# Where the first batch's rotation-table pieces and output weights stand in the load queue

## The chip, the cores and the metric

The kernel runs on one core of one Trainium2 chip. The metric is the device time of one execution in microseconds (us). The engines are named as in the profile: PE is the matrix engine (PEld its weight loads), DVE the vector engine, ACT the scalar engine, POOL the GpSimd engine, SP the engine whose queue issues every DMA of this kernel, in program order.

## The reference, cut to what matters

Two layers work on an image batch `x` of shape 8 x 256 x 96 x 96 in float32. The change touches only the first layer, and only for the first batch element:

```python
# layer 0, after a group norm of x
q_f = fft2(pconv(x, w1, b1)); k_f = fft2(pconv(x, w2, b2)); v_f = fft2(pconv(x, w3, b3))
q_f, k_f = l2_normalize(q_f), l2_normalize(k_f)          # per head, over all frequencies
attn = einsum('bhcn,bhdn->bhcd', q_f, k_f) * temperature
attn = complex(softmax(real(attn)), softmax(imag(attn)))
out  = abs(ifft2(einsum('bhcd,bhdn->bhcn', attn, v_f)))
x    = x + pconv(out, w_out)
# layer 1, after another group norm of x: linear attention with softplus features, added to x
```

No transform is carried out in full. The attention needs only sums over pairs of image rows (x with itself, and x with its mirrored image), and the absolute value of the inverse transform needs each image and a rotated copy of it.

## The kernel before

Each batch element passes through five stages, which Python generators interleave into one program. The order of instructions on every engine, SP included, is the order in which they are written, since the kernel schedules by hand.

- Pair sums. `first_sums` (first batch element only) turns 12 steps of two image rows each on PE, and `pair_sums(0)` does the rest, from row group u = 6 on. A row group is loaded by `load_grouped` (eight DMAs, L161 and L163, for two row groups), transposed on DVE in `turn_blocks` (L502), stored to the DRAM buffer `xtd` (L507), added and subtracted on POOL and DVE in `pair` (L529, L530), and multiplied on PE in `products` (L458), three block steps for each row group and one for the last, u = 12. The generator `rest` is `pair_sums(0)`: after its four preparing steps it yields after each block step, so that the index i of the loop `for i, _ in enumerate(rest)` counts 19 block steps, i = 0 to 18. The last row group is transposed at L489 and L491 and stored to `xtm` (L492).
- Tables. `tables()` builds a rotation table and writes it to the DRAM buffer `rx` (L283, L284) in 13 pieces for later reading; then it prepares small constants (`gsel`, `rep4`, `sel8`, L290 to L297) and hands over to `load_small`, which loads biases and weights. The output weights `wo` are loaded there: one DMA for the first half (L230), and 16 of 8 KB each for the second (L232), four of them between two yields. `parts` is this generator; each `next(parts)` runs it to its next yield.
- Rotation. `rotate(b)` returns `fetch`, which names or loads the next row pair and, when it is the first of a piece, loads the piece of the table from `rx` into a tile `tm` (L750, 159 KB, four buffers), and a generator of 49 steps (`turns`). A step multiplies rows by the piece on PE (L795) and copies the result to an image buffer (L801, L802) on ACT or DVE in turn. A piece serves four steps. Before step i, `steps` fetches ahead to row pair i // 2 + 3, so that step 0 fetches row pairs 0 to 3 (pieces 0 and 1), step 2 piece 2, step 6 piece 3, step 10 piece 4, step 14 piece 5 and step 18 piece 6. The first 12 row pairs of the first batch element are still in SBUF from `first_sums`; from pair 12 on they are loaded from `xtd` (L781) into slots that earlier pairs leave.
- Attention. `attention(b)` is a chain of small operations that yields the number of turns to be placed between two of its links. `mix(b, chain, turns)` does that.
- Images, then the second layer (`images`, `layer1`, `output`): the products with `wo` are at L864.

In the block steps of the first batch element, two turns each are run at i = 9, 10 and 11 and one each from i = 12 on (steps 0 to 12); the remaining turns are run in `mix`.

The DMAs of SP around the change thus stand in this order: store of row groups 6 and 7, eight loads, store of 8 and 9, six small loads of the last row group (L155, L156), pieces 0 and 1, store of 10 and 11, pieces 2 and 3, the store to `xtm`, the small loads, the weights `wl` (L452), five loads of `wo`, piece 4, twelve loads of `wo`, pieces 5 and 6, row pairs from `xtd`.

Of the kernel before, what the change touches and what calls it, by code (L numbers as in the profile page):

```python
# [73 lines left out]
def two_layer_kernel(ctx: ExitStack, tc: tile.TileContext, x, w1t, b1, w2t, b2, w3, b3, wot, temp,  # L74
# [139 lines left out]
    def load_small():  # L214
        nc.gpsimd.memset(b12[0:64], 0.0)
        yield
        for c, v in enumerate((b1, b2)):
            for m in range(KC):
                nc.sync.dma_start(out=b12[32 * m:32 * m + 1, c, :], in_=v[m * P:(m + 1) * P].unsqueeze(0))
        yield  # L220
        for c, v in enumerate((bk, bq)):
            nc.sync.dma_start(out=bkq4[:, c:c + 1], in_=bass.AP(v.tensor, v.offset, [[0, 4], [1, 32], [1, 1]]))
        for k in range(KC):
            nc.sync.dma_start(out=tcol[:, k:k + 1], in_=bass.AP(temp.tensor, temp.offset + 4 * k, [[1, 4], [0, HEAD], [1, 1]]))
        yield
        for c, v in enumerate((wkt, wqt)):
            nc.sync.dma_start(out=wkq0[:, :, c, :], in_=v.rearrange("(k p) o -> p k o", p=P))
        nc.sync.dma_start(out=b3col, in_=b3.rearrange("(k p) -> p k", p=P))
        yield
        nc.sync.dma_start(out=wo[:, 0, :], in_=bass.AP(wot.tensor, wot.offset, [[C, 16], [HEAD * C, NH], [1, C]]))  # L230
        for j in range(16):
            nc.sync.dma_start(out=wo[NH * j:NH * j + NH, 1, :], in_=wo_v[HEAD - j if j else 16])  # L232
            if j % 4 == 3:
                yield


    csn = const.tile([P, 3, H], F32, name="csn")
# [17 lines left out]
    def tables():  # L255
# [40 lines left out]
        nc.vector.tensor_copy(sel8.rearrange("p (i d) -> p i d", d=D), rep4[:, 0:8].unsqueeze(2).to_broadcast([P, 8, D]))  # L296
        nc.vector.tensor_scalar_mul(csn[:, 0:2, N + 1:H], csn[:, 0:2, N + 1:H], -1.0)  # L297
        yield from load_small()

    def tm_tile(name):  # L300
# [35 lines left out]
    def finish(stage):  # L336
        for _ in stage:
            pass
# [19 lines left out]
    def first_loads():  # L358

        nc.sync.dma_start(out=t0[:, 0:2 * W], in_=tmat[0, :, W:3 * W])  # L360
        x0 = x_of(0)

        def load(lo, hi):
            o = LO if hi <= H // 2 else 0
            nc.sync.dma_start(out=x0[:, :, o + lo * W:o + hi * W], in_=x_v[0, :, :, lo * W:hi * W])

        for lo, hi in ((0, 4), (H - 4, H), (4, 8), (H - 8, H - 4), (8, 16), (H - 16, H - 8)):
            load(lo, hi)
        yield
        load(16, 2 * NU)  # L370
        yield
        load(H - 2 * NU + 1, H - 16)
        load_grouped(0, V0)
        yield
        load_grouped(0, V0 + 1)
        yield
# [338 lines left out]
    def b3_part(b):  # L715

        pg = ps_tile(f"b3_{b}")
        mz, nmean, at = m0.pop(b)
        atf = at.rearrange("p m n h -> p m (n h)")
        for c in range(3):  # L720
            for j, r in enumerate(blocks(c)):
                for k in range(KC):
                    nc.tensor.matmul(pg[r, c:c + 1], lhsT=columns(atf, k, c, j), rhs=b3col[:, k:k + 1],
                                     start=(c == 0 and k == 0), stop=(k == KC - 1), skip_group_check=True)
        beta = one.tile([P, 3], F32, tag="beta", name=f"beta_{b}")
        nc.vector.tensor_copy(beta, pg[:, 0:3])
        m0[b] = mz, nmean, beta
# [372 lines left out]
    def weave(stage, other):  # L1100

        due = 0
        for n in stage:
            due += n
            while due >= 1:
                next(other, None)
                due -= 1
# [68 lines left out]
                        next(mixed)  # L1176
                        next(mixed)

    def mix(b, chain, turns):

        for n in chain:
            for _ in range(n):
                next(turns, None)
                yield
        nc.vector.tensor_copy(y1[b][:, :, H:H + 1], m0[b][1].unsqueeze(2))
        for _ in turns:
            yield
        b3_part(b)

    E = mybir.EngineType  # L1190
    with tc.manual_schedule(engines={E.PE, E.DVE, E.Pool, E.SP, E.Activation}):
        sums, rest, loads, parts = first_sums(), pair_sums(0), first_loads(), tables()
        fetch, turns = rotate(0)
        next(loads)
        next(parts)
        next(loads)
        next(parts)
        next(loads)
        next(parts)
        finish(loads)  # L1200
        for i, _ in enumerate(sums):
            if NU - 5 < i < NU:
                next(rest)
        for i, _ in enumerate(rest):
            if i > 11:
                next(parts, None)
            for _ in range(2 if i in (9, 10, 11) else 1 if i > 11 else 0):
                next(turns)
        finish(parts)
        finish(mix(0, attention(0), turns))  # L1210
        for b in range(B):
            sums = pair_sums(b + 1) if b + 1 < B else iter(())
            weave(images(b), sums)
            weave(layer1(b), sums)
            if b + 1 < B:
                fetch, turns = rotate(b + 1)
                mixed = mix(b + 1, attention(b + 1), turns)
                output(b, *l1.pop(b), fetch, sums, mixed)
                finish(mixed)
            else:  # L1220
                output(b, *l1.pop(b))
# [50 lines left out]
```

## Time and profile before

| | |
|---|---|
| median of 3 runs | 2518.16 us (2516.88 to 2520.02) |
| the profiled execution | 2517.75 us |
| its span | 2516.0 us |
| PE busy | 2476.9 us (98%) |
| PE busy from 0 to 149 us, all that precedes the images of the first batch element | 132.88 us |
| PE busy from 149 to 2420 us | 2263.96 of 2271 us |
| mean granted PE clock from 0 to 149 us | 0.95 of full speed |

The profile is one execution. A time such as 70.5 counts from the start of its span. PE, DVE, ACT and POOL times are those of instructions; SP times are those of issuing a DMA, which moves its data later. A remark in brackets behind an instruction is the time for which its engine stood idle before it, and what ended that. The program order on each engine is fixed[...].

### The profile page before, as it was taken

To read this page: it belongs to the slowest core of one execution; us is meant where nothing else is said; L and a number is where in the kernel's file an instruction comes from. 1 tells how busy PE (TensorE), PEld (TensorE's weight loads), DVE (VectorE), ACT (ScalarE), POOL (GpSimd) and SP (SyncE) were. 2 spreads that over 40 slices of the span, in tenths; PEclk is the share of its full clock that TensorE was granted. 3 is DMA by queue.
4 is the path that set the end of the run, shared out by engine and by line. 5 is a ranking of instruction groups with operands and counts; after the bars stand their busy time and mean duration, and the time that the engine had idled before them with its cause. 6 is when DMAs were issued, how large, how long until landed. Compare 5 with 4: busy or idle time off the path is not lost. (4 is left out here: it accounts for less than half of the span.)

```text
span 2516.0 us, 41727 instructions
## 1 busy us (share of the span) xinstructions
PE 2476.9 (98%) x15788; PEld 1745.1 (69%) x15788; DVE 1777.8 (71%) x3450; ACT 1148.2 (46%) x2007; POOL 856.6 (34%) x806
## 2 busy tenths in 40 slices
PE   9899999999999999999999999999999999999998
PEld 8775768667685667856678566785677757777546
DVE  5467776687856877578775787757876577766776
ACT  2244364443545445354453535435354453634553
POOL 5024513245133442144331452413524136142311
PEclk9899999999999999999999999999999999999997
DMA  9544619356292653916559263683638627296004
GB/s 242 152 154 105 174 64 331 139 137 174 72 336 93 168 143 118 339 63 158 135 173 327 49 166 97 230 271 63 163 86 284 216 63 197 53 318 207 1 7 151
DMA packets 274786, 403.79 MB, mean 160 GB/s; under 512 B 39670, under 2 KB 202906, under 8 KB 274586
## 3 DMA queue, kind: packets, MB, share of 16 engines
q1 hardware_dynamic: 274586, 401.11, 54.3%
q8 instruction: 126, 2.06, 0.4%
q14 instruction: 74, 0.61, 0.1%
HBM read 251.90 MB, written 149.14 MB: 159 GB/s over the span
## 5 line engine op out<-in xcount | busy, mean ns | idle before, releaser
L856 PE MATMUL z<-arena,mz 128*128 128x384 f32 (+1 forms) x2304 | 591.9, 488 | 0.0
L906 POOL TENSOR_TENSOR e<-e 128x768 f32<-128x768 f32 x192 | 348.4, 1814 | 552.6 <-ACT e L905 525.8
L864 PE MATMUL po<-e,wo 128*128 128x384 f32 x1536 | 527.5, 487 | 1.6 <-ACT e L907 1.6
L856 PEld LDWEIGHTS z<-arena,mz 128*128 128x128 f32 (+1 forms) x2304 | 310.1, 163 | 234.7 <-issue 50.5
L864 PEld LDWEIGHTS po<-e,wo 128*128 128x128 f32 x1536 | 290.0, 190 | 204.6 <-ACT e L907 7.2
L458 PEld LDWEIGHTS acc<-eo 128*128 128x128 f32 (+1 forms) x2224 | 353.2, 190 | 81.6 <-issue 32.3
L901 DVE TENSOR_TENSOR e<-z,xT 128x768 f32<-128x768 f32 x384 | 361.1, 949 | 66.0 <-PE z L856 65.8
L458 PE MATMUL acc<-eo 128*128 128x257 f32 (+3 forms) x2224 | 400.0, 330 | 0.0
L795 PEld LDWEIGHTS y<-tm,arena 96*128 96x128 f32 x3072 | 363.6, 193 | 49.8 <-issue 34.5
L795 PE MATMUL y<-tm,arena 96*128 96x128 f32 x3072 | 382.5, 279 | 11.4 <-DMA tm<-rx 11.4
L905 ACT ACTIVATE e<-e 128x1536 f32<-128x1536 f32 x192 | 284.4, 1481 | 174.4 <-DVE e L901 172.5
L866 DVE TENSOR_TENSOR arena<-arena,po 128x384 f32<-128x384 f32 x384 | 209.2, 551 | 181.2 <-PE po L864 181.2
L907 ACT ACTIVATE e<-e 128x768 f32<-128x768 f32 x192 | 161.9, 843 | 380.6 <-POOL e L906 376.7
L529 POOL TENSOR_TENSOR eo<-arena 128x768 f32<-128x768 f32 x83 | 172.1, 2074 | 433.2 <-DVE arena L502 332.7
L1161 POOL TENSOR_TENSOR arena<-arena,po 128x384 f32<-128x384 f32 x180 | 178.0, 1008 | 197.5 <-ACT po L1160 153.2
L801 ACT COPY arena<-y 128x384 f32<-128x384 f32 (+1 forms) x200 | 94.5, 473 | 259.6 <-PE y L795 240.8
L801 DVE COPY arena<-y 128x384 f32<-128x384 f32 (+1 forms) x192 | 104.6, 545 | 144.2 <-PE y L795 142.8
L304 DVE BATCH_NORM_STATS2 st<-arena 128x6 f32<-128x384 f32 x384 | 195.1, 548 | 0.6
L502 DVE STREAM_TRANSPOSE arena<-arena 128x768 f32<-128x768 f32 x180 | 166.1, 955 | 8.9 <-DMA xtd<-arena 7.0
L1160 ACT COPY po<-o 128x384 f32<-128x384 f32 x180 | 78.0, 482 | 191.8 <-PE o L1152 186.8
L1021 PE MATMUL xT<-ident,arena 128*128 128x128 f32 x1152 | 144.1, 275 | 1.3 <-ACT xT L1024 1.3
L1021 PEld LDWEIGHTS xT<-ident,arena 128*128 128x128 f32 x1152 | 127.1, 141 | 19.0 <-issue 16.5
(244 smaller groups left out, 2540.6 us busy)
## 6 DMA issues: line engine op xcount, KB each, us to landing
arena<-in_x_dram SPq DMA_DIRECT2D x99, 768.0 KB
out_dram<-arena SPq DMA_DIRECT2D x192, 384.0 KB
xtd<-arena SPq DMA_DIRECT2D x45, 1536.0 KB
arena<-xtd SPq DMA_DIRECT2D x180, 384.0 KB
arena<-in_x_dram SPq DMA_DIRECT2D x353, 192.0 KB
tm<-rx SPq DMA_DIRECT2D x96, 159.0 KB
wl<-in_w1t_dram SPq DMA_DIRECT2D x8, 256.0 KB
wl<-in_w2t_dram SPq DMA_DIRECT2D x8, 256.0 KB
```

The lines of the kernel that those rows point to most:

```text
L304: nc.vector.bn_stats(out=st[:, k, c, :], in_=x_of(b)[:, k, c * CH:(c + 1) * CH])
L458: nc.tensor.matmul(acc[c][:, m * (C + 1):m * (C + 1) + C + 1 - m * P], lhsT=eo[0:np_, q, c, 1 + m * P:1 + (m + 1) * P], rhs=eo[0:np_, q, c ...
L795: nc.tensor.matmul(pu[:, o:o + P], lhsT=xt[:, s, k * P:(k + 1) * P], rhs=tm[:, n:n + P], start=True, stop=True)
L801: copy(y[:, :, :, g:g + nr, :], v.rearrange("p k r (f w) -> p k f r w", f=2))
L856: nc.tensor.matmul(out[:, 0:CH].rearrange("p (h q) -> p h q", q=PR), lhsT=columns(mz, k, c, j), rhs=yz[:, k, f, :, o:o + PR], start=(k == ...
L864: nc.tensor.matmul(po[:, 0:CH], lhsT=wo[:, k, m * P:(m + 1) * P], rhs=e[:, k, :], start=(k == 0), stop=(k == KC - 1))
L866: nc.vector.tensor_add(x[:, m, n], x[:, m, n], po[:, 0:CH])
L901: nc.vector.tensor_add(e[:, 2 * c:2 * c + 2, :].rearrange("p t (q h) -> p t q h", h=H), pz[:, 0:CH].rearrange("p (h q) -> p q h", h=H).uns ...
L905: nc.scalar.activation(e, e, AF.Square)
L906: nc.gpsimd.tensor_add(e[:, 0:2, :], e[:, 0:2, :], e[:, 2:4, :])
L1021: nc.tensor.transpose(pt[:, j * C + k * P:j * C + (k + 1) * P], x[:, k, o:o + P], ident)
L1161: nc.gpsimd.tensor_add(x[:, m, r], x[:, m, r], t)
```

## The change

Three edits, none of which changes what is computed. The fetching of the first four row pairs, and with them of table pieces 0 and 1, is placed after the first block step (i = 0), where before it came with the first turn at i = 9. `load_small` yields after each of the 16 small loads of `wo` and not after every fourth. `parts` begins one block step later (i = 13), and what is left of it after the block steps is run inside `mix`, one `next(parts)` for each turn, where before it was run to its end ahead of `mix`.

```diff
         for j in range(16):
             nc.sync.dma_start(out=wo[NH * j:NH * j + NH, 1, :], in_=wo_v[HEAD - j if j else 16])
-            if j % 4 == 3:
-                yield
+            yield
...
-    def mix(b, chain, turns):
+    def mix(b, chain, turns, parts=iter(())):
 
         for n in chain:
             for _ in range(n):
                 next(turns, None)
+                next(parts, None)
                 yield
...
         for i, _ in enumerate(rest):
-            if i > 11:
+            if i == 0:
+                for _ in range(4):
+                    fetch()
+            if i > 12:
                 next(parts, None)
             for _ in range(2 if i in (9, 10, 11) else 1 if i > 11 else 0):
                 next(turns)
+        finish(mix(0, attention(0), turns, parts))
         finish(parts)
-        finish(mix(0, attention(0), turns))
```

## The prediction

> **What bounds the kernel now.** I read the page's busy times first, then PE's waits over the whole span, then the order of work on PE and on the SP queue between 55 and 112 us, then windows over the stretches where PE stops.
>
> The page and PE's waits (columns: us in total, times, longest):
>
> ```profile
> PE 2476.9 (98%) x15788; PEld 1745.1 (69%) x15788; DVE 1777.8 (71%) x3450; ACT 1148.2 (46%) x2007; POOL 856.6 (34%) x806
> ...
> PE y L795 <- DMA tm<-rx: 11.4, 3, 6.8
> PE pcs L259 <- POOL xo L424: 3.6, 1, 3.6
> PE gm_b L316 <- DVE mv_b L310: 2.7, 1, 2.7
> ```
>
> PE is busy for all but 39 us. The largest wait is that of the rotation's matmuls for pieces of the rotation table (tm): three times, 11.4 us together. They are on PE's timeline:
>
> ```profile
> 59.77 3.89 PE L458 MATMUL acc<-eo 128*128 128x257 f32 x23
> 70.50 2.90 PE L795 MATMUL y<-tm,arena 96*128 96x128 f32 x12 [6.84 <-DMA tm<-rx]
> 73.19 1.94 PE L458 MATMUL acc<-eo 128*128 128x257 f32 x8
> ...
> 94.42 3.73 PE L795 MATMUL y<-tm,arena 96*128 96x128 f32 x32
> 98.74 2.92 PE L795 MATMUL y<-tm,arena 96*128 96x128 f32 x24 [0.59 <-DMA tm<-rx]
> ...
> 107.13 5.98 PE L795 MATMUL y<-tm,arena 96*128 96x128 f32 x32 [4.02 <-DMA tm<-rx]
> ```
>
> The SP queue shows why the pieces are late (start, duration, transfer, how many):
>
> ```profile
> 56.95 1.57 SPq L163 DMA_DIRECT2D arena<-in_x_dram  x1
> 58.62 0.40 SPq L507 DMA_DIRECT2D xtd<-arena  x1
> ...
> 65.00 3.98 SPq L750 DMA_DIRECT2D tm<-rx  x2
> ...
> 91.98 1.53 SPq L232 DMA_DIRECT2D wo<-in_wot_dram  x4
> 93.62 0.79 SPq L750 DMA_DIRECT2D tm<-rx  x1
> 94.45 5.79 SPq L232 DMA_DIRECT2D wo<-in_wot_dram  x12
> 100.34 1.25 SPq L750 DMA_DIRECT2D tm<-rx  x2
> ```
>
> Pieces 0 and 1 are issued at 65.0, after PE already stands (63.66), and behind a 1.5 MB store (xtd) and six small loads. Piece 4 stands behind five wo loads, piece 5 behind twelve more. Each gap also costs clock:
>
> ```profile
> 67.00:70.50 3.50, 0.00 (x0) 0.03 (x1) 0.89 (x1) 0.00 (x0) 2.60 (x2) 0.54 0.38 88
> 70.50:74.00 3.50, 3.50 (x14) 3.36 (x15) 0.56 (x3) 0.54 (x2) 0.00 (x0) 0.50 0.12 43
> 104.90:108.30 3.40, 1.17 (x5) 1.20 (x6) 0.00 (x0) 0.00 (x0) 0.00 (x0) 0.50 0.82 193
> 108.30:111.70 3.40, 3.40 (x18) 3.40 (x17) 0.63 (x2) 0.54 (x2) 0.00 (x0) 0.50 0.21 34
> ```
>
> The third number from the right is the granted clock: 0.50 from about 67.3 to 74.1 and from about 104.9 to 111.7.
>
> [...] the second fall came 1.75 us after PE stopped, in a window that had been about half busy. [...] The window 69:72, where only tm moves, has DMA share 0.20[...]. [...]
>
> **The change, part by part.** A piece of 159 KB moves at 68 to 88 GB/s: 2.2 us.
>
> *First pieces at the head of the block steps.* The four fetches come after block step 0 of row 6: on SP just behind the eight loads that end at 58.52, ahead of the store at 58.62. Two DMAs move; the other two fetches only name tiles. Nothing is added. The source rx was written from 30 to 36 us. SP waits here fit a rule that a transfer waits for the eighth before it (the second tm waited 2.4 us for the xtd store, eight places earlier), so pieces 0 and 1 wait for the first two of the eight loads, done by about 59: issue at 58.7 and 59.2. [...] whose bytes end between 63 and 64 (DMA share 1.16 at 207 GB/s in 58:63; DVE's wait for them ends at 64.60). Then 2.2 us, then about 0.4 to the start of PE: 65.5 to 66.5. I take 66.0. The gap from 63.66 shrinks from 6.84 to 2.3: **4.5 us gained**, between 3.0 and 6.8. Piece 1 lands near 68; it is needed 6 us after piece 0.
>
> What is pushed back: the xtd store by two issues (about 1.5 us)[...]. Then the six small loads, whose reader runs on DVE at 83[...]. What else is due: row 10's sums need eo, made on POOL from 66.97 to 69.55 and untouched; PE would want it 7.5 us after it starts again, at 73.5. Covered.
>
> *Clock after the first gap.* The first group ran 12 matmuls in 2.90; at full clock 8 take 1.06 and each further 0.111, so 1.50: loss 1.40. The next eight products took 1.94 instead of 1.48: 0.46. Together 1.86. With 2.3 us of idle the clock may or may not fall[...] (idle of 1.75 in one window was enough at 104.9). I take half: **0.9 gained**, between 0 and 1.86.
>
> *wo one per turn.* Ahead of piece 4 went wo's first load and four more, 91.33 to 93.62: 2.29 us; they leave, and the small loads go one step later. The transposes of the last block also pass in front of the twelve gsel copies and six more DVE instructions (L290 to L297, 81.47 to 83.31, 1.84 us), so the xtm store on which SP waited until 83.84 comes earlier. Piece 4 is thus 4.1 us earlier against PE; it was 0.59 late. Ahead of piece 5, 5.89 us of wo (94.45 to 100.34) become one load of 0.61 and three of 0.48, 2.05: 3.84 more, 8.0 in all, against 0.59 + 4.02 of lateness. **0.59 and 4.02 gained**, and with them the half clock at 107.13: 32 matmuls in 5.98, where 94.42 has 3.73 for as many: **2.25 gained**.
>
> The other wo loads lie between later turns, 0.48 on SP for each turn of at least 1.06 us on PE. From turn 22 on SP waits for PE (row loads into slots that PE frees); seven wo between turns 20 and 26 delay those by at most 3.4 us, and such a row, issued at 110.52, is read near 117.8 with about 3 us of transfer: some 4 us of cover. First reader of wo is at 160, over 40 us later. The copies moved one step (gsel, read at 142.9; b12, at 114.2) are early enough; without that cover they would cost their 1.9 us on DVE. The chain of attention keeps its place: at 102.83 its last small matmul, 1.5 us later its result, and four turns (4.2 us) before PE needs it.
>
> Sum: 4.5 + 0.9 + 0.59 + 4.02 + 2.25 = 12.3 us. The profiled execution took 2517.75 (span 2516.0 and 1.75 around it), so 2505.4; the median shown is 0.4 higher: **2505.8**. From 149 to 2420 us PE is busy for 2264 of 2271, so what is gained at the head should reach the end whole.
>
> **Rivals.**
> - *The wait moves to piece 2.* [...] PE wants it 13.2 us after it starts again (70.50 to 85.58, less 1.86), at 79. For it: the margin is one microsecond[...]. Against it: piece 3 is not needed before 87. Two microseconds late and a halved clock cost 3 to 4: 2509.5.
> - *The first pieces land no earlier in effect*[...]: only the second part pays, 6.86: 2511.3. Against it, nothing but the eight loads is ahead of them.
> - *The chain takes the gaps' place, no change:* its waits would have to take 12 us; the 1.5 us above against 4.2 speaks against it.
> - *Slower:* wo loads in the turns hold SP while row loads queue behind; each of the eleven row loads from 110 us on would come late. It decides from 4 us of delay per load; 2 us late at all eleven, each with a piece of half clock, would be 22 + 4, less 12: 2532. Only seven wo are left by then, and SP stands idle in its waits for PE (26 us of them), which speaks against it.
>
> **Chances.** Forecast 0.62; wait at piece 2 0.19; second part alone 0.11; no change 0.04; slower 0.04. The forecast's own range is 2502 (first gap all gone with its clock: 15.6 gained, 2502.6) to 2508; to hold the rivals of the same sign it goes to 2512. A measurement tells about 0.2%, 5 us, from no change: faster 0.92, same 0.04, slower 0.04.
>
> **What would show it.** PE's wait L795 for tm falls from 11.4 to 2 or 3 us, in one piece near 64; on SP, two tm issues near 59 ahead of the xtd store, wo loads one by one between tm and row loads; clock 1.00 from 104 on. Wrong: a wait for tm at PE's step 8 (near 79 us), a wait for xtd rows after 105, or a first gap that stays over 4 us.

## The result, and the profile after

The changed kernel takes 2504.23 us (median of 4 runs, 2503.14 to 2505.93) beside 2517.52 us for the kernel before: the ratio is 0.9947, with a 95% interval of 0.993 to 0.9964, or 13.3 us less. The profiled execution of the changed kernel has a span of 2502.6 us, 13.4 us less than that of before. In the changed file the lines behind the loads of wo (L232) are one lower, so that L794 is the rotation's matmul, L749 the load of a table piece and L506 the store of a row group.

PE's waits over the whole span of the changed kernel (us in total, times, longest):

```profile
PE pcs L258 <- POOL xo L423: 3.6, 1, 3.6
...
PE y L794 <- DMA tm<-rx: 1.8, 1, 1.8
```

Three waits of 11.4 us for table pieces have become one of 1.8. On PE's timeline of the changed kernel:

```profile
65.97 1.73 PE L794 MATMUL y<-tm,arena 96*128 96x128 f32 x12 [1.85 <-DMA tm<-rx]
67.49 2.78 PE L457 MATMUL acc<-eo 128*128 128x257 f32 x8
70.06 2.24 PE L794 MATMUL y<-tm,arena 96*128 96x128 f32 x16
...
80.97 1.06 PE L794 MATMUL y<-tm,arena 96*128 96x128 f32 x8
...
89.81 6.42 PE L794 MATMUL y<-tm,arena 96*128 96x128 f32 x56
...
97.54 3.82 PE L794 MATMUL y<-tm,arena 96*128 96x128 f32 x32
101.29 1.03 PE L589 MATMUL qkm<-wl,dmm 128*2 128x256 f32 x8
```

Read it for three things. The first turn starts at 65.97 after a gap of 1.85 us. The group behind it is slow (2.78 where 1.48 is usual). From 89.81 on there is no gap at all: 56 matmuls in one line where the kernel before had 32, a wait and 24, and the 32 at 97.54 take 3.82 instead of 5.98. The SP queue of the changed kernel:

```profile
59.22 1.67 SPq L749 DMA_DIRECT2D tm<-rx  x2
60.99 0.42 SPq L506 DMA_DIRECT2D xtd<-arena  x1
...
86.00 0.80 SPq L749 DMA_DIRECT2D tm<-rx  x1
86.85 0.59 SPq L230 DMA_DIRECT2D wo<-in_wot_dram  x1
87.49 1.74 SPq L232 DMA_DIRECT2D wo<-in_wot_dram  x3
89.32 0.77 SPq L749 DMA_DIRECT2D tm<-rx  x1
```

Pieces 0 and 1 stand ahead of the store now, piece 4 ahead of all of wo, and piece 5 behind four loads of it.

Where did the 13.4 us of the two profiles come from? Two marks on PE cut every execution the same way: the first matmul on a finished rotation (zs, in `images`) ends the head, which holds all that the change touches, and the first matmul of the last group norm (gm_b of the last batch element) begins the end, where PE waits often.

| profiled execution | to zs, us | zs to last gm_b | last gm_b to the end |
|---|---|---|---|
| before | 147.64 | 2277.20 | 91.16 |
| changed | 135.89 | 2277.24 | 89.47 |
| changed_again (below) | 135.13 | 2277.27 | 91.20 |

The head gives 11.75 us, the middle passes it on unchanged, and 1.7 us come from the end, which the change doesn't touch. There the mean granted clock was 0.92 instead of 0.80 in the last 95 to 97 us. In the third row, the same kernel executed again, the end is as long as before, so those 1.7 us belong to the execution and not to the change.

### The profile page after: what moved, and what is told of

It is laid out like the page before. It is cut to its first block, busy times and chain, and to the rows that moved or that the text cites. A ratio compares the mean times of both kernels' runs of the same rounds, so it can differ in the third digit from the quotient of the medians.

```text
span 2502.6 us, 41727 instructions
## 1 busy us (share of the span) xinstructions
PE 2468.9 (99%) x15788; PEld 1735.1 (69%) x15788; DVE 1777.3 (71%) x3450; ACT 1148.1 (46%) x2007; POOL 856.8 (34%) x806
## 5 line engine op out<-in xcount | busy, mean ns | idle before, releaser
L794 PEld LDWEIGHTS y<-tm,arena 96*128 96x128 f32 x3072 | 360.6, 192 | 40.4 <-issue 27.1
L794 PE MATMUL y<-tm,arena 96*128 96x128 f32 x3072 | 379.3, 278 | 2.1 <-DMA tm<-rx 1.8
```

What stands on the lines that cost most here:

```text
L794: nc.tensor.matmul(pu[:, o:o + P], lhsT=xt[:, s, k * P:(k + 1) * P], rhs=tm[:, n:n + P], start=True, stop=True)
```

## Experiments

My theory was that the pieces came late for two separate reasons, one for each part of the change; that only their place in SP's queue and the transfers ahead of them count; and that a wait costs its length and, at times, a stretch of half clock (6.8 us at 0.50 after two of the three gaps of the kernel before, 3.4 us after the gap of the changed one). Eleven runs follow, one of them the changed kernel once more. Times stand as ratios to the kernel before on the same chip, with 95% intervals; these reach 2 to 3.5 us to either side. Line numbers shift by the lines that an edit adds.

### One part at a time

```diff
 # pieces_only: the kernel before, and
+            if i == 0:
+                for _ in range(4):
+                    fetch()
 # wo_only: the changed kernel without these three lines
```

> Only the early fetch is made; the output weights stay as before (four small loads between two yields, run to the end ahead of the attention chain). My theory (two separate sets of late table pieces): the first wait of PE for tm shrinks from 6.84 us to about 1.9, the clock still falls after it, and the two later waits with their half clock (0.59 + 4.02 + 2.25 us) stay: about 4.5 us less than before, 2513. Rival (the early pieces make everything behind them early too, so that one part is enough): the later waits are gone as well, 2506 or below.

> Only the spreading of the output weights is made; pieces 0 and 1 are fetched with the first turn as before. My theory: the first wait stays at 6.8 us with its half clock, the two later waits are gone with theirs: about 6.9 us less than before, 2510.6. Rival (both parts needed together, since with the first wait in place the later ones move elsewhere): a wait for tm or for row pairs remains after 90 us, 2514 or above.

Measured: pieces_only 0.9977 (0.9968 to 0.9986), 5.8 us less than before; wo_only 0.9969 (0.9957 to 0.9981), 7.8 us less by its ratio. PE's timeline of pieces_only:

```profile
66.78 2.16 PE L795 MATMUL y<-tm,arena 96*128 96x128 f32 x12 [2.84 <-DMA tm<-rx]
...
95.20 2.92 PE L795 MATMUL y<-tm,arena 96*128 96x128 f32 x24 [0.85 <-DMA tm<-rx]
...
102.71 6.60 PE L795 MATMUL y<-tm,arena 96*128 96x128 f32 x32 [3.14 <-DMA tm<-rx]
```

The first gap is short and the two later ones are there, with the slow 32 matmuls. PE's timeline of wo_only has the first gap alone:

```profile
73.09 2.90 PE L794 MATMUL y<-tm,arena 96*128 96x128 f32 x12 [9.01 <-DMA tm<-rx]
...
98.13 6.42 PE L794 MATMUL y<-tm,arena 96*128 96x128 f32 x56
...
109.61 1.03 PE L589 MATMUL qkm<-wl,dmm 128*2 128x256 f32 x8
```

Its gap is 2.2 us longer than in the kernel before, though nothing ahead of it differs. SP's waits of wo_only show why: before issuing the eight row loads it waited longer for the store of row groups 6 and 7 (5.9 us in the kernel before).

```profile
SPq L161 <- DMA xtd<-arena: 8.2, 1, 8.2
```

So the landing of that store varies by 2 us from one execution to another. The two parts are separate, as the timelines show: from the turns ahead of the second gap to the matmuls qkm of the attention chain, pieces_only took 18.63 us, as the kernel before did, and wo_only 11.48, as the changed kernel did. That stretch of the kernel before ends with

```profile
113.04 1.03 PE L590 MATMUL qkm<-wl,dmm 128*2 128x256 f32 x8
```

The times agree with that as far as they go: 5.8 and 7.8 add to 13.6, against 13.3 for both, with intervals of 2 to 3 us on each part.

### Only the place in the queue counts

```diff
 # position_3: the changed kernel, with
-            if i == 0:
+            if i == 3:
 # wo_last: the changed kernel, with
-        finish(mix(0, attention(0), turns, parts))
+        finish(mix(0, attention(0), turns))
         finish(parts)
```

> As the changed kernel, but the four fetches come after block step 3 instead of block step 0. No DMA is written between these two places, so the order of SP's queue is the same. My theory (only the place in SP's queue counts): the same time within 0.1%, 2504, and pieces 0 and 1 issued at the same times near 59. Rival (the program's place counts for itself): a later issue and a longer first wait, 2507 or more.

> As the changed kernel, but the fourteen small loads of the output weights that are left after the block steps are issued behind all turns instead of one per turn. My theory (what counts is that they leave the way of pieces 4 to 6; they are needed some 20 us later): the same time within 0.1%, 2504, and no wait of PE for wo. Rival (late weights are waited for, or they hold the image loads that follow): a wait at the first products with wo near 148 us, 2506 or more. Rival on the other side (wo between the turns still costs): faster by 1 us or more.

Measured: position_3 0.9946 (0.9932 to 0.9959), the same as the changed kernel; its pieces are issued at 58.19, again behind the eight loads. wo_last 0.9942 (0.993 to 0.9955), 2502.92 us: its fourteen loads are issued from 123.50 on, and PE's first product with wo starts after a gap of no more than 0.2 us. What helps is thus that wo leaves the way of the pieces, not that it goes one load per turn. Whether the loads between the turns cost a microsecond is not settled, since the intervals overlap.

### What sets the gap that is left

The prediction put 2.2 us of piece 0's lateness down to its own transfer, 159 KB in one DMA at 68 to 88 GB/s. A window of the kernel before, in which only pieces move (the last two numbers are DMA share and GB/s):

```profile
69.00:72.00 3.00, 1.50 (x7) 1.53 (x8) 0.00 (x0) 0.00 (x0) 0.60 (x2) 0.50 0.20 60
```

A share of 0.20 of 16 engines is 3.2: a piece kept about three engines busy, an estimate from that share. Two edits test what the form of the piece costs, alone and together: three DMAs of 32 partitions for a piece, and an earlier place.

```diff
 # three_dmas: the changed kernel, with
+                for q in range(NQ):
+                    nc.sync.dma_start(out=tm[32 * q:32 * q + 32, 0:o], in_=v[q])
+                return tm
 # earlier: the changed kernel with the fetches ahead of the store and the eight loads
+            if i == NU - 2:
+                for _ in range(4):
+                    fetch()
             if NU - 5 < i < NU:
                 next(rest)
 # slot: the changed kernel with the fetches in turn_blocks, between the store and the eight loads
                 nc.sync.dma_start(out=xtd[:, v].rearrange("c p m -> p c m"), in_=turned_flat(b, u))
+                if b == 0 and u == 2 * V0 + 1:
+                    for _ in range(4):
+                        fetch()
 # slot_three: slot and three_dmas
```

> As the changed kernel, but each of pieces 0 to 5 is loaded by three DMAs of 32 partitions instead of one with a slowest dimension of 3. My theory [...]: [...] PE's first wait falls from 1.85 us to 0.5 or less, the clock does not fall, 3 us less than the changed kernel: 2501. The stretch in which only tm moves at a DMA share of 0.2 is gone. Rival (the wait is set by the eight row loads ahead and by the landing, not by the number of engines): the wait stays at 1.5 us or more, 2504, and the longer issue on SP shows.

> As the changed kernel, but pieces 0 and 1 are fetched ahead of the store of row groups 6 and 7 and of the eight row loads, some 12 us earlier. My theory (only the transfers ahead of the pieces hold them): PE's first wait for tm is gone. But [...] these end 2 to 4 us later, and row group 10, on which PE has some 2 us of cover, comes late: a wait of up to 2 us for its sums near 72 us. Net 0 to 3.5 us less than the changed kernel, 2500.5 to 2504. Rival (the eight loads are bound elsewhere and lose nothing): full gain of 3.7 us, 2500.5.

Measured: three_dmas 0.9943 (0.993 to 0.9955), not to be told from the changed kernel; my theory had 3 us. SP's and PE's timelines of three_dmas:

```profile
57.80 5.82 SPq L750 DMA_DIRECT2D tm<-rx  x6
```

```profile
65.65 1.58 PE L797 MATMUL y<-tm,arena 96*128 96x128 f32 x12 [1.05 <-DMA tm<-rx]
```

Six issues take 5.82 us; three of them wait for row loads ahead, 2.5 us together. The turn starts at 65.65, which is 0.3 us sooner than in the changed kernel (65.97), and 0.8 to 1.1 us sooner than in the other four executions with the same order and one DMA for a piece (pieces_only, position_3, wo_last and changed_again below: 66.42 to 66.78). The gap of 1.05 us lies between my theory (0.5 or less) and the rival (1.5 or more). The clock did not fall (1.00 from 60 to 90 us), and the head took 133.91 us, where it took 134.74 to 136.36 in the four of these that have both parts of the change (changed, position_3, wo_last and changed_again). So behind the eight loads, which DVE had at 64.9, the form of the piece is worth less than the 2.2 us that the prediction put down to it, but the traces do not show it to be nothing.

earlier: 0.9952 (0.9939 to 0.9964), about 1 us slower than the changed kernel by its ratio, with intervals that overlap; its head is clearly longer, 139.82 us. PE's timeline of earlier:

```profile
63.55 1.50 PE L794 MATMUL y<-tm,arena 96*128 96x128 f32 x12
...
71.66 1.13 PE L794 MATMUL y<-tm,arena 96*128 96x128 f32 x8 [1.30 <-DVE ys L801]
...
81.67 2.04 PE L794 MATMUL y<-tm,arena 96*128 96x128 f32 x8 [2.77 <-DMA tm<-rx]
```

The first gap is gone. But the eight row loads went out at 57.75 instead of 54.07, because they wait for the store of row groups 6 and 7. That the pieces ahead of it made the store late was not shown: SP waited 9.9 us for it, and 8.2 us in wo_only, where no piece was ahead of it. Row group 10 reached DVE at 67.88 instead of 64.50. DVE's copies of the turns stand behind it (1.30 us), and so do the next store and piece 2 (2.77 us, with half clock after it: 8 matmuls in 2.04 us where 1.06 is usual). This is the rival "the wait moves to piece 2" of the prediction, brought about by a further advance.

> As the changed kernel, with pieces 0 to 5 in three DMAs of 32 partitions each, and pieces 0 and 1 issued right behind the store of row groups 6 and 7, where SP waits some 6 us for that store before it may issue the eight row loads. My theory (the pieces must be out of the way of the eight loads without holding them or the later pieces): no wait for tm at the first turn and none later, no fall of the clock, row group 10 as early as in the changed kernel (transposes near 64.5 to 65): 3.5 us less than the changed kernel, 2500.5 on the same scale. Rival (each advance of the first turns only uncovers the next wait, row group 10 or piece 2): a new wait of 2 us or more between 70 and 85 us, 2503 or above.

> As slot_three, but with each piece in one DMA whose slowest dimension is 3. My theory [...]: no wait at the first turn, [...] row group 10 and with it the store of row groups 10 and 11 and piece 2 come later, and PE waits for piece 2 at step 8 for 1 to 3 us with half a clock after it: 2503 to 2506, no better than the changed kernel. Rival (number of engines does not matter): as slot_three, 2500.5.

Measured: slot_three 0.9939 (0.9927 to 0.9951), slot 0.996 (0.9947 to 0.9972). DVE's timeline of slot, and of slot_three, where it takes up row group 10:

```profile
68.75 0.17 DVE L496 COPY wrap<-arena 128x16 f32<-128x16 f32 x1 [11.21 <-DMA arena<-in_x_dram]
```

```profile
64.21 0.17 DVE L496 COPY wrap<-arena 128x16 f32<-128x16 f32 x1 [8.03 <-DMA arena<-in_x_dram]
```

The two differ only in the form of the pieces, and row group 10 comes 4.5 us later with one DMA for each piece ahead of it. Of this, 3.2 us are later issue: the eighth row load is out at 61.75 us, where it is out at 58.55 in slot_three, and SP waited 1.7 us for a piece ahead of it. slot then waits 1.7 us for DVE and 2.8 us for piece 2; slot_three starts the first turn at 63.30 without a gap and waits 0.80 us at step 8. PE's timeline of slot_three:

```profile
63.30 1.50 PE L800 MATMUL y<-tm,arena 96*128 96x128 f32 x12
```

The five times of slot, 2506.39 to 2509.72 us, all lie above the five of slot_three beside it, 2500.84 to 2504.06. So the form of the pieces does matter, and more for what stands behind them than for the pieces themselves. Whether this comes from the few engines that a piece keeps busy (about three, by the estimate above) or from the number of DMAs was not shown: no run isolates it.

### A better version, and the clock

```diff
 # changed_again: the changed kernel
 # three_and_last: slot_three and wo_last
 # three_last_late: three_and_last, with
-            if i > 12:
+            if i > 14:
                 next(parts, None)
```

> The changed kernel once more, on the same chip as the next two and as a second look at its first gap. My theory (the gap before the first turn is some 1.9 us in each execution[...]): the gap is 1.5 to 2.3 us again; the clock either falls to half for 3.4 us or not at all, and the head is 1.8 us shorter in the second case. Time 2503 to 2506. Rival (gap and fall are set by the program): clock falls at the same place, 67.2 us, by the same amount.

> Three DMAs per piece, pieces 0 and 1 in SP's wait for the store, and the last fourteen loads of the output weights behind all turns. My theory: as with the first two alone, since the weights are out of the way in either place: no wait at the first turn, one of about 0.8 us near 77, 2 us less than the changed kernel on the same chip. Rival (weights between the turns cost something): another 1 us or more.

> As three_and_last, with the small tables' copies on DVE and the small loads two block steps later, and all seventeen loads of the output weights behind the turns. If the wait of 0.8 us at step 8 comes from DVE (its copies stand behind the transposes that wait for the store of row groups 10 and 11), it is gone: up to 0.8 us less than three_and_last. If it is the landing of piece 2, it stays as it is. A wait for the biases or tables in the attention chain, which now come later, would show as PE waiting near 110 to 130 us and cost what it lasts.

Measured on one chip: changed_again 0.9944 (0.9932 to 0.9957), three_and_last 0.9934 (0.9922 to 0.9947), three_last_late 0.993 (0.9917 to 0.9944). The last two are at 2501.4 us, 4.0 us less than the changed kernel beside them; the intervals of the ratios still overlap. The heads agree with a gain: 132.53 us in slot_three, 132.33 in three_and_last and 133.94 in three_last_late, against 134.74 to 136.36 in the four executions with both parts and the pieces behind the eight loads. The wait at step 8 came and went: 0.80 us in slot_three, none in three_and_last, and in three_last_late, where DVE's copies are out of the way, PE's timeline shows

```profile
78.95 1.13 PE L800 MATMUL y<-tm,arena 96*128 96x128 f32 x8 [1.40 <-DMA tm<-rx]
```

So in this one it is the landing of piece 2, not DVE. That of slot_three, which the profile put down to a DVE copy, was not settled.

The clock: windows of the changed kernel, and of the same kernel in changed_again (the third number from the right is PE's granted clock):

```profile
67.00:70.50 3.50, 3.50 (x16) 3.12 (x16) 2.90 (x5) 0.00 (x0) 2.96 (x3) 0.54 0.43 112
70.50:74.00 3.50, 3.50 (x28) 3.39 (x28) 0.63 (x2) 0.99 (x4) 1.60 (x2) 0.98 0.98 380
```

```profile
67.00:70.50 3.50, 3.50 (x30) 3.39 (x29) 3.40 (x6) 0.00 (x0) 2.65 (x2) 1.00 0.55 155
70.50:74.00 3.50, 3.50 (x30) 3.39 (x29) 0.83 (x3) 1.19 (x5) 2.05 (x2) 1.00 0.82 305
```

The gap was 1.85 us in the first and 2.75 us in the second, and the clock fell after the shorter one. PE's timelines of changed_again, position_3 and wo_last have these gaps:

```profile
66.55 1.58 PE L794 MATMUL y<-tm,arena 96*128 96x128 f32 x12 [2.75 <-DMA tm<-rx]
```

```profile
66.45 1.58 PE L794 MATMUL y<-tm,arena 96*128 96x128 f32 x12 [1.89 <-DMA tm<-rx]
```

```profile
66.42 1.58 PE L794 MATMUL y<-tm,arena 96*128 96x128 f32 x12 [2.00 <-DMA tm<-rx]
```

The length of the gap doesn't decide. What separates the cases is how much of it falls into one step of a grid: in each trace all changes of the granted clock lie on steps of 3.41 us, and the place of this grid against the span differs from one execution to the next:

| execution | gap, us | step of the grid with most of it | PE idle in that step, us | clock after it |
|---|---|---|---|---|
| changed | 1.85 | 63.85 to 67.26 | 1.85 | half |
| position_3 | 1.89 | 64.72 to 68.13 | 1.73 | half |
| pieces_only | 2.84 | 64.18 to 67.59 | 2.60 | half |
| wo_last | 2.00 | 62.64 to 66.05 | 1.63 | full |
| changed_again | 2.75 | 62.00 to 65.42 | 1.62 | full |

The gap of changed_again is cut by a boundary of the grid at 65.42, so that neither side holds more than 1.62 us of it. In all thirteen traces, from 10 to 150 us, the clock fell at the end of each of the nine steps in which PE, at full clock, stood idle for 1.73 us or more, about half of a step, and after no step with 1.63 us or less. It is not a rule for the whole kernel: after 2380 us, where PE does other work, the clock fell after a step with 1.47 us of idle (2480.53 to 2483.94, before) and stayed full after one with 1.82 (2408.80 to 2412.22, changed).

## Why the prediction was right

- *First gap, 2.3 us left and 4.5 gained.* Measured 1.85 left, with PE arriving 0.46 us later than in the profile of before: 6.84 - 1.85 - 0.46 = 4.53. The start at 66.0 was 65.97. The price of 2.2 us for the transfer of piece 0 was too high in this sum: without it, three_dmas started only 0.3 to 1.1 us sooner, so that the start at 66.0 was met partly by luck. That the eight loads ahead hold piece 0 fits slot_three, where the pieces stand ahead of them and the gap is gone; how the rest divides between loads and landing is open.
- *Clock after it, half of 1.86.* In the profiled execution the gain was 0.04: 12 matmuls in 1.73, products in 2.78, 16 matmuls in 2.24 lose 0.23 + 1.30 + 0.29 = 1.82. In changed_again it was nearly whole: 12 matmuls in 1.58, products in 1.48. To take half was fair for a mean; in one execution it is chance: in one and the same kernel, 1.85 us of idle fell into one step of the clock's grid in the first and 1.62 in the second.
- *wo out of the way, 6.86 us.* From the turn group before the second gap to qkm, 94.42 to 113.04, were 18.62 us; now, 89.81 to 101.29, they are 11.48: 7.14 gained. Most of the excess of 0.3 lies at the second gap: the matmuls on its two sides took 3.73 and 2.92 us and take 6.42 as one group. The margins were smaller than forecast, and enough: against PE, piece 4 was issued 3.0 us earlier where 4.1 was forecast, and piece 5 6.4 where 8.0 was.
- *Sum for the head, 12.3.* 4.53 + 0.04 + 7.14 = 11.71; the marks say 11.75. The forecast of 12.3 is nearer to this than its terms are: the clock gave 0.04 of its 0.9, and the later gaps 0.3 more than put. The prediction of 2505.8 missed the median by 1.6 us, within what the clock in the head and at the end moves an execution, and the interval of the measured gain, 9 to 17.6 us, does not tell 12.3 from 11.7.
- *What passes on.* The middle is the same to 0.04 us. The end was not reckoned with: 89.0 to 91.2 us over the thirteen profiled executions of this study.
- *The wait at piece 2* did not come in the changed kernel: step 8 starts at 80.97 without a wait, with PE held up by the clock as well. In changed_again, where the clock did not fall, it starts at 80.14, some 0.2 us behind its usual place. The margin of one microsecond was the author's estimate; that it was thin shows in earlier and slot, which waited 2.77 us each for piece 2.
- *Second part alone* was run as a kernel of its own: 0.9969, or 2510.4 on the scale of the prediction, where 2511.3 was forecast.
- *No change* and *slower* found nothing: PE does not wait for the attention chain or for row pairs anywhere in the head.

## What to carry to other kernels

A queue that issues all transfers in order has a critical order of its own: small loads that nobody needs for a long time cost their issue time when they stand ahead of one that PE is about to need (5.79 us for the twelve loads of wo ahead of piece 5), and nothing that could be measured here when they stand behind it (0.9947 with them between the turns, 0.9942 with them behind all turns). Before moving a load forward, ask what stands behind it: a table piece as one DMA started the first turn 0.3 to 1.1 us later than the same piece in three DMAs when it stood behind the eight row loads, and cost 5 us of the whole when it stood ahead of them (0.996 against 0.9939). The shortest heads, 132.33 and 132.53 us, had the pieces in three DMAs each, in the stretch in which the queue itself stood waiting.

## What was not expected of the hardware

The granted clock fell after gaps of 1.85 and 1.89 us and did not after 2.00 and 2.75 us, in kernels that have the same order of loads up to there; these two falls lasted 3.4 us each. What separated them was how much of the gap fell into one step of a grid of 3.41 us. The landing of one 1.5 MB store moved by 2.3 us between executions (SP waited 5.9 or 8.2 us for it), and the end of the kernel by 2.2 us (89.0 to 91.2), both with nothing changed in the program that bears on them.
